# A four-layer graph network in one kernel: order of emission held on four engines, LSTM gates from Tanh alone

## The chip, the cores and the metric

The kernel runs on one core of one Trainium2 chip. The metric is the device time of one execution in microseconds; the time before is 2408.22 us, the median of three runs (2407.28 to 2410.26). Lower is better. All data are float32.

A core has a TensorE (PE in the profile; its weight loads are shown as PEld), which multiplies matrices from SBUF into PSUM; a VectorE (DVE), a ScalarE (ACT) and a GpSimd (POOL), which work element by element; and a SyncE (SP), whose queue issues most of the DMAs here. Each engine takes its instructions in the order of its own queue, and an instruction that needs another engine's result waits on a semaphore.

## The reference

The input is 128 graphs of 64 nodes with 256 features each, and one adjacency matrix. Four layers follow; each ends in `x = layernorm(x + layer(x))`.

- **Layer 0**: nodes are mixed by a normalised adjacency, then 256 to 512 features, a batch norm over all graphs and nodes, ReLU, 512 to 256, and a second batch norm. The batch norms need all data before any of it can go on.
- **Layer 1**: nodes are mixed by a scaled Laplacian, a linear map, layernorm (g1, be1), ReLU and residual; attention with four heads; layernorm (g2, be2); a feed-forward part with GELU; layernorm (g3, be3). The Laplacian is scaled by its largest eigenvalue, which the kernel finds by repeated squaring.
- **Layer 2**: two graph convolutions, and then four passes of LSTMs over windows of the 64 nodes: for p = 1, 2, 3, 4 in turn, each window of p consecutive nodes is run through an LSTM with weights of its own, and the result replaces the window's last node.
- **Layer 3**: graph attention with one head.

The LSTM step, cut to what the change touches:

```python
g = x_t @ Wih.T + h @ Whh.T + bias
i, f, gg, o = jnp.split(g, 4, axis=-1)
c = jax.nn.sigmoid(f) * c + jax.nn.sigmoid(i) * jnp.tanh(gg)
h = jax.nn.sigmoid(o) * jnp.tanh(c)
```

## The kernel before

**Tiling.** The data are 16 blocks of 512 rows (8 graphs of 64 nodes), each a tile of 128 x 1024 elements. Two layouts are in use: rows on the partitions (four pieces of 128 x 256) or features on the partitions (two pieces of 128 x 512). PSUM holds four tiles of 128 x 1024; SBUF holds the blocks and eight further tiles of that size, and tiles of blocks that are done are lent out as further ones.

**The planner.** All work is written as Python generators, one for each block or unit of work, which run while the kernel is built. Before each step a generator yields `step(engine, us, ...)` with the step's engine (T, V, S, G for TensorE, VectorE, ScalarE, GpSimd; Q for a DMA), a length in us from a table of costs written by hand, and the PSUM and SBUF tiles that it takes. `flow` (line 130) keeps a planned time for each engine. From all generators in progress it picks the step that could start first, where a step counts as ready only when its inputs have been due for a margin (line 30: 2.0 us for T, 0.5 for V and S), and among equals the one of the stream with the lowest priority number. It then lets that generator emit its instructions. The order of emission is thus the planner's order. Before the queues are filled, the framework under the kernel sorts the instructions once more, so an engine's queue need not be in the order of emission.

A step on the ScalarE whose `tbl` differs from the last one is planned 1.3 us longer, for the load of another table of functions: the three in use are named "gelu", "exp" and "sigmoid".

**Streams.** A first `flow` does layer 0 (`first_block`, `second_block`, between them the batch norms) and the eigenvalue (`eig`). A second `flow` does all the rest, with several streams side by side, each with a width (generators at a time) and a priority: `end_block` (the end of layer 0) and `block` (layer 1) in one stream of width 6; `gcn_block` (the convolutions and the LSTM for p = 1) of width 2; the LSTM units for p = 2 to 4 of width 2, except the last three, which have a stream of their own with width 1, priority 1.5 and `urgent`, which sets the margin aside; the weights' loads; and layer 3 (`last_block`) for the first 12 blocks with priority 6 and, cut into eight half blocks, for the last 4 blocks with priority 2. The last three units are the last group of graphs for p = 4, in two halves, and the group before it.

**Layernorm** comes in three forms. All begin with `stats` (line 265): for each of four pieces a `bn_stats` (L272) and a `bn_aggr` (L273), then one addition of epsilon (L274), all on the VectorE; then GpSimd raises the variance to the power -0.5.

- `ln_steps` (without weights) applies it on the VectorE (L285).
- `ln_affine_steps` (with weights; GpSimd at L294) applies it on the VectorE with two instructions for each piece, L297 and L300.
- `ln_steps_act` (GpSimd at L308) has one small VectorE instruction (L311) for minus mean times factor, and applies it on the ScalarE, one instruction for each piece (L314).

In `block` the layernorms g1 and g3 use the second form, g2 the first, and the last one the third.

**LSTM.** `lstm` (line 1025) does the first step of a window, where there is no h yet: the matmuls at L1055, the gates on the ScalarE with Sigmoid or Tanh (L1067), the product of i and g on GpSimd (L1086), tanh of the cell on the ScalarE (L1094), and the product with o on the VectorE (L1102, or straight into the block at L1357 and L1389). Later steps of whole units use a form of Strassen's scheme with seven products of half size (L1127), evictions at L1165 to L1195, gates at L1203 to L1207, a product on GpSimd (L1220) and the cell's update on the VectorE (L1228, L1231). Units of half the graphs take `plain_steps` (line 1250), with L1264 and L1266 as matmuls, L1269 as gates, L1280 on GpSimd, and L1282, L1284, L1296 on the VectorE.

**Other lines that the prediction names**: L341 the mixing of nodes, with matmuls of a quarter of the array; L353 and L359 transposes; L365 and L377 the products with weights; L749 and L772 evictions with an addition; L784 the copy of the transposed block; L808 the values; L822, L915, L916 and L933 GpSimd's additions and products with rows of weights over whole blocks; L852 a subtraction in the softmax; L898 the eviction after the attention; L928 GELU; L938 the second feed-forward product; L1325, L1345 evictions and L1353 the second ReLU in `gcn_block`; in `last_block` L1467 the copies of h, L1478 the addition of h, L1492 and L1494 copies, L1507 the product with the weights, L1519 an eviction, L1536 to L1540 the scores, L1544 the exponentials, L1555 a copy.

## Time and profile before

| what | us |
|---|---|
| median of three runs | 2408.22 |
| profiled execution | 2409.44 |
| its span, first to last instruction | 2407.7 |
| TensorE busy | 2287.2 |
| VectorE busy | 1287.7 |
| ScalarE busy | 1187.4 |
| GpSimd busy | 591.7 |

The profile comes from one execution. A row of a group reads: line, engine, operation, what it writes and reads (with the numbers of tiles left out), sizes as partitions x elements, how often; then its busy time and the mean length of one in ns; then the engine's idle time just before and what ended it. A row of waits reads: the engine and its line, what it waited for, the sum in us, how often, the longest. A row of a timeline begins with the start in us from the span's start and the length. In a table of windows each row is a stretch of time with the busy time of each engine; PEclk is the mean clock that the TensorE was granted, as a share of the full one. A TensorE that shows as busy need not be at its full rate, since the ends of its instructions are modelled.

By time, the work lies so: layer 0 up to about 270 us; the end of layer 0, layer 1, the convolutions and the first LSTM pass up to about 1290; the LSTM units for p = 2 to 4 with layer 3 of the first blocks up to about 2150; the last units and the rest of layer 3 to the end.

### The profile page before, as it was taken

To read this page: it belongs to the slowest core of one execution; us is meant where nothing else is said; L and a number is where in the kernel's file an instruction comes from. 1 tells how busy PE (TensorE), PEld (TensorE's weight loads), DVE (VectorE), ACT (ScalarE), POOL (GpSimd) and SP (SyncE) were. 2 spreads that over 40 slices of the span, in tenths; PEclk is the share of its full clock that TensorE was granted. 3 is DMA by queue.
4 is the path that set the end of the run, shared out by engine and by line. 5 is a ranking of instruction groups with operands and counts; after the bars stand their busy time and mean duration, and the time that the engine had idled before them with its cause. 6 is when DMAs were issued, how large, how long until landed. Compare 5 with 4: busy or idle time off the path is not lost.

```text
span 2407.7 us, 40603 instructions
## 1 busy us (share of the span) xinstructions
PE 2287.2 (95%) x16916; PEld 1759.9 (73%) x16916; DVE 1287.7 (53%) x2904; ACT 1187.4 (49%) x2189; POOL 591.7 (25%) x441
## 2 busy tenths in 40 slices
PE   8999788999989999999999999999999999998997
PEld 4548665666665666666667788899999888887785
DVE  4557678566483474744643433454444444455546
ACT  2257643544434544335453443444444653468766
POOL 0012134232242232331321222222221222122122
PEclk9999899999999999999999999999999999999998
DMA  6100301000000000001000000000001000001111
GB/s 162 49 1 1 111 23 49 28 10 10 1 12 17 10 10 10 1 10 36 36 19 27 18 1 1 17 2 1 1 1 36 1 10 9 19 27 66 40 36 45
DMA packets 42633, 57.91 MB, mean 24 GB/s; under 512 B 6224, under 2 KB 35536, under 8 KB 42448
## 3 DMA queue, kind: packets, MB, share of 16 engines
q1 hardware_dynamic: 41344, 54.22, 7.0%
q8 instruction: 133, 2.18, 0.4%
q10 hardware_dynamic: 1104, 1.08, 0.1%
q14 instruction: 52, 0.43, 0.1%
HBM read 38.52 MB, written 16.78 MB: 23 GB/s over the span
## 4 chain that ended last, share of the span: by engine, by line
PE 60%; DVE 16%; ACT 7%; POOL 3%; issue 2%; POOLq 0%; ACTq 0%; DVEq 0%
PE ps L1127 26%; PE ps L1055 11%; PE ps L365 7%; PE ps L377 4%; PE ps L938 4%; DVE ln_st L272 3%; ACT x L314 2%; PE ps L808 2%; POOL ln_rs L308 1%; PE ps L1507 1%; DVE x L300 1%; PE ps L341 1%; DVE ln_mv L273 1%; PE ps L353 1%; DVE ln_nm L311 1%
## 5 line engine op out<-in xcount | busy, mean ns | idle before, releaser
L1127 PE MATMUL ps<-x,x 128*128 128x256 f32 x928 | 225.0, 380 | 0.7 <-DVE t L1195 0.7
L1127 PEld LDWEIGHTS ps<-x,x 128*128 128x128 f32 x928 | 173.5, 190 | 24.9 <-issue 1.6
L314 ACT ACTIVATE x<-x,ln_nm,ln_rs 128x256 f32<-128x256 f32 x212 | 112.3, 592 | 133.3 <-DVE ln_nm L311 131.9
L1127 PE MATMUL ps<-t,x 128*128 128x256 f32 x672 | 163.7, 380 | 0.0
L1127 PEld LDWEIGHTS ps<-t,x 128*128 128x128 f32 x672 | 126.4, 190 | 17.1 <-DVE x L1195 0.8
L308 POOL TENSOR_TENSOR ln_rs<-ln_rs,neghalf 128x4 f32<-128x4 f32 (+1 forms) x72 | 71.2, 990 | 212.0 <-DVE ln_rs L274 186.4
L365 PE MATMUL ps<-t,W1T 128*128 128x512 f32 x256 | 117.8, 607 | 0.0
L1055 PE MATMUL ps<-h,wL 128*128 128x192 f32 (+2 forms) x480 | 103.9, 371 | 4.8 <-ACT h L1353 4.8
L272 DVE BATCH_NORM_STATS2 ln_st<-x 128x6 f32<-128x256 f32 x260 | 99.7, 403 | 0.4
L1055 PEld LDWEIGHTS ps<-h,wL 128*128 128x128 f32 x480 | 75.6, 192 | 29.9 <-issue 22.5
L294 POOL TENSOR_TENSOR ln_rs<-ln_rs,neghalf 128x4 f32<-128x4 f32 x32 | 36.9, 1153 | 217.1 <-DVE ln_rs L274 217.0
L1055 PE MATMUL ps<-h,x 128*128 128x256 f32 x384 | 86.7, 380 | 2.2 <-ACT t L1067 1.8
L1067 ACT ACTIVATE t<-ps,bih 128x512 f32<-128x512 f32 (+3 forms) x98 | 57.2, 634 | 55.8 <-PE ps L1055 55.1
L1203 ACT ACTIVATE x<-x,bih 128x512 f32<-128x512 f32 (+2 forms) x69 | 44.6, 648 | 80.3 <-DVE x L1193 80.0
L1186 DVE COPY x<-ps 128x256 f32<-128x256 f32 (+2 forms) x69 | 26.1, 378 | 108.4 <-PE ps L1127 107.6
L365 PEld LDWEIGHTS ps<-t,W1T 128*128 128x128 f32 x256 | 47.6, 195 | 49.6 <-issue 49.5
L365 PE MATMUL ps<-t,wA 128*128 128x512 f32 x160 | 76.8, 626 | 5.5 <-ACT t L784 5.5
L1055 PEld LDWEIGHTS ps<-h,x 128*128 128x128 f32 x384 | 72.6, 190 | 12.9 <-ACT t L1067 2.2
L1186 DVE COPY t<-ps 128x256 f32<-128x256 f32 (+2 forms) x51 | 18.8, 373 | 103.8 <-PE ps L1127 103.5
L1067 ACT ACTIVATE x<-ps,bih 128x512 f32<-128x512 f32 (+3 forms) x86 | 51.5, 650 | 40.6 <-PE ps L1055 40.4
L273 DVE BATCH_NORM_AGGREGATE ln_mv<-ln_st 128x2 f32<-128x6 f32 x448 | 71.3, 167 | 0.0
L1193 DVE TENSOR_TENSOR x<-ps,x 128x512 f32<-128x512 f32 (+2 forms) x69 | 41.4, 602 | 53.0 <-PE ps L1127 43.6
(714 smaller groups left out, 5713.2 us busy)
## 6 DMA issues: line engine op xcount, KB each, us to landing
t<-in_x_dram SPq DMA_DIRECT2D x26, 512.0 KB, 4.3
xd<-x SPq DMA_DIRECT2D x16, 512.0 KB, 2.6
x<-xd SPq DMA_DIRECT2D x8, 512.0 KB, 3.3
out_dram<-x SPq DMA_DIRECT2D x8, 512.0 KB, 2.9
h<-in_x_dram SPq DMA_DIRECT2D x5, 512.0 KB, 5.2
wL<-in_L_gnn_Wih_dram SPq DMA_DIRECT2D x2, 1024.0 KB, 5.0
x<-in_L_gnn_Whh_dram SPq DMA_DIRECT2D x2, 1024.0 KB, 5.4
x<-xd SPq DMA_DIRECT2D x5, 256.0 KB, 2.9
```

The lines of the kernel that those rows point to most:

```text
L272: V.bn_stats(st[:, t, :], y[:, t, :])
L273: V.bn_aggr(mv[:, t, :], st[:, t, :])
L308: G.tensor_tensor(rs, rs, neghalf[:, :n], ALU.pow)
L314: S.activation(y[:, t, :], y[:, t, :], AF.Identity, scale=rs[:, t : t + 1], bias=nm[:, t : t + 1])
L365: T.matmul(ps[:, c, :], w[:, k, (off + c) * P : (off + c + 1) * P], yT[:, k, :], start=(k == 0), stop=(k == nk - 1),)
L377: T.matmul(ps[:, t, :], yT[:, k, t * P : (t + 1) * P], w[:, k, :], start=(k == 0), stop=(k == nk - 1),)
L808: T.matmul(pv[r * N : (r + 1) * N, b, :, :], x1T[:, k, b * N : (b + 1) * N], Wv_par[:, k, r, :, :], start=(k == 0), stop=(k == 1),)
L938: T.matmul(tm(PS[ps])[:, t, :], fm(mem[gs[k // 2]])[:, k % 2, t * P : (t + 1) * P], W2[:, k, :], start=(k == 0), stop=(k == 3),)
L1055: T.matmul(spread(fm(PS[ps])[:, j, :n], q), WL[p][0][:, k, m], x_of(0, q)[:, k], start=(k == 0), stop=(k == 1),)
L1067: S.activation(of(sl)[:, j], fm(PS[ps])[:, j, :n], AF.Tanh if g == 2 else AF.Sigmoid, bias=bias(g, c))
L1127: T.matmul(dst, WS[p][name](k, g), y[:, k], start=first and k == 0, stop=k == 1, skip_group_check=not first)
L1186: V.tensor_copy(y[:, 1, :], v[:, 0, :])
```

## The change

1. **Order held.** `tc.manual_schedule` for TensorE, VectorE, ScalarE and GpSimd: the framework's sorting is off for these four, and each queue is in the order of emission. SP isn't among them.
2. **The planner.** The margin for T is 0.5 instead of 2.0 in the second flow. Its clocks start at the time at which the first flow ended. Many lengths are changed by some per cent. Steps have further marks: on the VectorE "m" for an instruction with two inputs from SBUF, on GpSimd "m" for one over a large tile; a VectorE step marked "m" is planned no earlier than the end of the last GpSimd step marked "m". On the TensorE a change between forms of matmul ("quarter", "columns", or neither) is planned 0.1 us longer. There is a list `DRAWS` with which margins can be multiplied by drawn numbers; it is empty, and every factor is 1.
3. **Layernorms g1 and g3** use `ln_steps_act`, followed by one multiplication and one addition over the whole block; `ln_affine_steps` is gone.
4. **LSTM.** Sigmoid of z is computed as (1 + tanh(z/2))/2, with the halves left out: the cell and h are kept at twice their value. A gate is Tanh with a scale of 0.5 or 1, halved again where the inputs are doubled; a product with a gate is (gate + 1) times the other, in one instruction; the cell's update has a factor of 0.5. All products are on the VectorE, and GpSimd keeps only differences. The bias is scaled once, in `gcn_rows`. `last_block` takes half of h.
5. **Streams.** The last three units are in the common stream of the units (width 2, priority 5), and the half blocks of the last group have priority 5.5 instead of 2.

```diff
-MARGIN = {"T": 2.0, "V": 0.5, "S": 0.5}
+MARGIN = {"T": 0.5, "V": 0.5, "S": 0.5}
+STRETCH = 50.0
+DRAWS = []
...
+    E = mybir.EngineType
+    ctx.enter_context(tc.manual_schedule(engines={E.PE, E.DVE, E.Activation, E.Pool}))
...
+                if e == "V" and tbl == "m":
+                    t, soon = max(t, locked), max(soon, locked)
...
-            if tbl is not None and tbl != table:
+            if e == "S" and tbl is not None and tbl != table:
                 us, table = us + 1.3, tbl
+            if e == "T" and tbl != shape:
+                us, shape = us + 0.1, tbl
+            if e == "G" and tbl == "m":
+                locked = when + us
...
-        yield step("V", 2.45)
+        yield step("V", 2.43)
         mv, rs = stats(y)
...
-    def ln_affine_steps(y, g, b):
-
-        yield step("V", 2.45)
-        mv, rs = stats(y)
-        yield step("G", 1.0)
-        G.tensor_tensor(rs, rs, neghalf[:, :NT], ALU.pow)
-        yield step("V", 3.4)
-        for t in range(NT):
-            V.scalar_tensor_tensor(y[:, t, :], y[:, t, :], mv[:, t, 0:1], g, ALU.subtract, ALU.mult)
-            o = b if len(b.shape) == 2 else b[:, t, :]
-            dst = y if len(b.shape) == 2 else b
-            V.scalar_tensor_tensor(dst[:, t, :], y[:, t, :], rs[:, t : t + 1], o, ALU.mult, ALU.add)
...
-        yield step("V", 0.6 * n)
+        yield step("V", 0.3 + 0.53 * n)
         mv, rs = stats(y)
...
-        yield from ln_affine_steps(y, rows[:, names.index("g1"), :], rows[:, names.index("be1"), :])
-        yield step("V", 1.25)
+        yield from ln_steps_act(y)
+        yield step("V", 3.7, tbl="m")
+        V.tensor_tensor(y, y, row["g1"], ALU.mult)
+        V.tensor_tensor(y, y, row["be1"], ALU.add)
         V.scalar_tensor_tensor(y, y, 0.0, x, ALU.max, ALU.add)
...
-        yield from ln_affine_steps(y, rows[:, names.index("g3"), :], x)
+        yield from ln_steps_act(y)
+        yield step("V", 2.45, tbl="m")
+        V.tensor_tensor(y, y, row["g3"], ALU.mult)
+        V.tensor_tensor(x, y, x, ALU.add)
...
-    V.tensor_tensor(bl, bl, bh, ALU.add)
...
+        V.tensor_tensor(bl, bl, bh, ALU.add)
+        for j in (slice(0, 4), slice(6, 8)):
+            V.tensor_scalar(bl[:, :, j], bl[:, :, j], 0.5, None, ALU.mult)
         mark("rows")
...
+        def gate(dst, z, g, c):
+            S.activation(
+                dst,
+                z,
+                AF.Tanh,
+                bias=bl[:, p - 1, 2 * g + c : 2 * g + c + 1],
+                scale=(1.0 if g == 2 else 0.5) * (1.0 if p == 1 else 0.5),
+            )
+
+        def times(dst, y, z):
+
+            V.scalar_tensor_tensor(dst, y, 1.0, z, ALU.add, ALU.mult)
...
-            t = yield step("G", g_us, at=t, waits=False)
-            G.tensor_tensor(of(s_cell)[:, c], of(sl)[:, 0], of(sl)[:, 1], ALU.mult)
+            t = yield step("V", v_us, at=t, waits=False, tbl="m")
+            times(of(s_cell)[:, c], of(sl)[:, 0], of(sl)[:, 1])
...
-            t_g = yield step("G", 2 * g_us, at=at[2], waits=False)
-            G.tensor_tensor(of(act[2]), of(act[0]), of(act[2]), ALU.mult)
+            t_g = yield step("V", 2 * v_us, at=at[2], waits=False, tbl="m")
+            times(of(act[2]), of(act[0]), of(act[2]))
...
-            V.tensor_tensor(cell, cell, of(act[2]), ALU.add)
+            V.scalar_tensor_tensor(cell, cell, 0.5, of(act[2]), ALU.mult, ALU.add)
...
-        V.tensor_tensor(x, px, x, ALU.add)
+        V.scalar_tensor_tensor(x, px, 0.5, x, ALU.mult, ALU.add)
...
-            Stream(4, 2, end),
+            Stream(4, 5.5, end),
             Stream(2, 3, gcn),
             Stream(6, 4, seq),
-            Stream(2, 5, units[:-3]),
-            Stream(1, 1.5, units[-3:], urgent=True),
+            Stream(2, 5, units),
             Stream(4, 6, last),
         ],
         MARGIN,
+        start=done["bn2",],
```

## The prediction

> **What bounds the kernel now.** I read the busy times first, then a table of windows cut where the picture changes, then what the TensorE waited for, and last the timelines around those waits. The profiled execution took 2409.4 us, 2407.7 of it span; the sum below is made against it, and it stands 1.2 us above the median of the runs, 2408.2.
>
> ```profile
> PE 2287.2 (95%) x16916; PEld 1759.9 (73%) x16916; DVE 1287.7 (53%) x2904; ACT 1187.4 (49%) x2189; POOL 591.7 (25%) x441
> ```
>
> ```profile
> core 0: us, PE busy (x) PEld busy (x) DVE busy (x) ACT busy (x) POOL busy (x), PEclk, DMA share, GB/s
> 270.00:430.00 160.00, 133.79 (x1272) 97.86 (x1273) 121.42 (x304) 83.79 (x123) 56.79 (x36) 0.90 0.17 52
> 430.00:660.00 230.00, 224.32 (x2264) 149.47 (x2263) 128.22 (x288) 109.63 (x141) 71.48 (x43) 0.99 0.04 13
> 660.00:740.00 80.00, 72.02 (x709) 46.89 (x705) 55.55 (x119) 33.94 (x44) 29.11 (x17) 0.94 0.04 14
> 960.00:1060.00 100.00, 90.64 (x987) 63.68 (x977) 74.36 (x137) 41.21 (x50) 43.23 (x24) 0.97 0.03 12
> 1290.00:1860.00 570.00, 568.71 (x3166) 515.25 (x3165) 250.37 (x449) 248.63 (x560) 127.35 (x91) 1.00 0.03 8
> 2150.00:2360.00 210.00, 195.01 (x1247) 161.77 (x1245) 111.72 (x385) 161.31 (x371) 42.01 (x51) 0.99 0.15 50
> 2360.00:2407.70 47.70, 30.17 (x208) 22.55 (x208) 28.23 (x124) 33.31 (x86) 10.14 (x16) 0.86 0.15 51
> ```
>
> The change removes no matmul, so only the 120 us in which the TensorE is idle, and the time at a lowered clock, can be won. From 270 to 1290 us (layers 1 and the start of 2) it is idle for 57.9 us, and three stretches that make a third of that time hold 43.6 of them: 26.2, 8.0 and 9.4. There the VectorE is busy for 76, 69 and 74%, against 53% in the rest, and PEclk falls to 0.90, 0.94 and 0.97. From 1290 to 2150 the TensorE is idle for under 5 us: the LSTM stage gives nothing. From 2150 on it is idle for 32.5 us, 17.5 of them in the last 47.7; the ScalarE is at 77% until then and at 70% in the last stretch.
>
> In the middle stage the TensorE's longest waits are for the VectorE and ScalarE (us, times, longest):
>
> ```profile
> PE ps L365 <- ACT t L784: 5.5, 1, 5.5
> PE ps L938 <- DVE t L898: 5.5, 1, 5.5
> PE ps L1055 <- ACT h L1353: 4.8, 2, 4.3
> ```
>
> The last of these, at 722 us, goes back to this (timelines of VectorE and GpSimd: start, length, group):
>
> ```profile
> 710.07 5.85 DVE L300 SCALAR_TENSOR_TENSOR x<-x,ln_rs,x 128x256 f32<-128x256 f32 x4 [0.51 <-POOL ln_rs L294]
> ```
>
> ```profile
> 710.01 2.34 POOL L822 TENSOR_TENSOR x<-x,rows 128x1024 f32<-128x1024 f32 x1
> 712.32 2.53 POOL L916 TENSOR_TENSOR h<-h,rows 128x1024 f32<-128x1024 f32 x1
> ```
>
> Four instructions whose usual length is 0.47 us each take 5.85 together while two GpSimd products run. Then the VectorE does another block's statistics before the eviction at L1345 on which the ReLU L1353 and the TensorE wait.
>
> **The change, part by part.**
>
> **Layernorm with weights.** Two of a block's layernorms (g1, g3) now go through the ScalarE. Removed per layernorm: eight VectorE instructions, L297 and L300. In 270 to 1290 these took 70.7 + 81.0 = 151.6 us for 32 layernorms, 4.74 each (3.8 at their medians of 0.474 and 0.48). Added: one L311 (0.43 with its stalls, 0.16 without) and two 128x1024 operations at 1.22 (L852 with two SBUF inputs: median 1.22, mean 1.36), 2.8 together; four L314 on the ScalarE at 0.592, 2.37. VectorE: 32 x 1.9 = 61 us less. ScalarE: 76 us more, hidden: it is busy for 472 of these 1020 us. A layernorm's own path is no shorter (4.74 before; 0.2 + 2.37 + 2.44 and one more hand-over after), so the gain is VectorE time only, not latency.
>
> **LSTM.** Products of gates go from GpSimd to VectorE: L1086, 1.27 us for 128x512, becomes about 0.69 (row L1102); L1220, 2.39, becomes 1.22 (row L1228); L1280, 0.73, becomes 0.42 (row L1282). In 270 to 1290 that is 32 x 0.69 = 22 us more VectorE and 41 us less GpSimd. The later ones stand under a TensorE that is 99% busy: 0; without that cover each would shorten its step by the difference, about 1 us in 24 cell updates. The doubled values cost nothing: every one of those instructions keeps its size and engine (a multiply becomes a three-operand form; 128x256 takes 0.42 either way, L1538 and L1536). The three small instructions that bring the bias to its new form (0.19 and twice about 0.16) are in a step that ends long before the first LSTM product at 453 us.
>
> **Order held.** In the profile the VectorE's order is not that of the code, where every L273 follows its own L272:
>
> ```profile
> 400.98 0.74 DVE L272 BATCH_NORM_STATS2 ln_st<-x 128x6 f32<-128x256 f32 x2
> 401.64 0.16 DVE L273 BATCH_NORM_AGGREGATE ln_mv<-ln_st 128x2 f32<-128x6 f32 x1
> 401.72 0.39 DVE L272 BATCH_NORM_STATS2 ln_st<-x 128x6 f32<-128x256 f32 x1
> 402.03 0.16 DVE L273 BATCH_NORM_AGGREGATE ln_mv<-ln_st 128x2 f32<-128x6 f32 x1
> ```
>
> One L272 always lies between, and so L273 starts 0.08 us before the instruction ahead of it ends. Where an instruction reads what the one just ahead wrote (L273 to L274, L1536 to L1538), it starts 0.035 after that end. Held order makes all 448 pairs such neighbours: 0.117 each, 0.47 per layernorm, and the evictions queued behind them (L749, L1345) come later by as much, with the TensorE waiting for those. The Trainium skill (VectorE: DVE Perf Modes, The DRAIN you can't avoid) says that the next operation waits for the pipe to empty anyway and that semaphores add nothing; by that this costs 0. The rows differ, and I take them: 320 pairs in 270 to 1290, 37 us more VectorE. Over that stage the VectorE then comes out even: -61 + 22 + 37 = -2. In the three tight stretches it does not: L297 and L300 take 76.3 us there for 14 layernorms, 39 after; 140 pairs cost 16; four LSTM products 3; in all 18 us less. What of it reaches the TensorE lies between 0 and all; I take 10, and 3 us for the clock that stays up (bounds 0 and 8).
>
> What the new order itself is worth is not in this trace. The code now keeps VectorE instructions with two SBUF inputs off GpSimd's long ones, counts the change of matmul shape, and lets a matmul group be chosen when its inputs are due 0.5 us ahead instead of 2.0. If nothing is better, 0; at best the other 48 us of idle time in this stage; at worst a loss (below). I take a third, 15, nearer to nothing, because the TensorE's waits are spread over 27 places. Layer 0 has no L272 and the same steps: 0. LSTM stage: 0, bounds -5 and +10.
>
> **Tanh alone.** Of 79 table loads 31 serve a sigmoid and 16 serve the exponentials of the last layer between them; 28 of the 29 after 2100 go.
>
> ```profile
> L1544 ACT ACT_TABLE_LOAD x14 | 18.0, 1283 | 3.2 <-DVE mx L1540 3.0
> L1269 ACT ACT_TABLE_LOAD x10 | 12.8, 1283 | 0.2
> ```
>
> ```profile
> 2158.49 1.28 ACT L1544 ACT_TABLE_LOAD   x1
> 2159.79 0.35 ACT L1544 ACTIVATE t<-t,mx 128x64 f32<-128x64 f32 x1
> ```
>
> The page ScalarE: Activation LUTs (What ACT_TABLE_LOAD costs) adds a drain of 1.38 us to each load; here the load follows an activation that ends 0.02 before and the next starts 0.02 after it, so 28 loads are 36 us, not 74. Its table of sets puts tanh beside exp, which the change needs; no run here shows it. In layer 1 it spares 16 to 32 more, off the path. At the end the ScalarE falls from 194.6 to about 161 of 257.7 us (26 of the loads lie there). The TensorE's waits for the ScalarE after 2150 sum to 12.2; half, 6. Three loads (2361.95, 2364.04, 2388.74) lie after or beside the last LSTM step: 3.8. The clock: 1. Longer statistics in two last layernorms: +0.5. Together -10; bounds -22 and +26.
>
> **The last units in the common stream.** They issue no DMA. They lose their rank over the last layer's blocks, whose loads (2.9 us) and stores go on SP, which is not held. What is queued behind them is the last four half blocks: counted as 0, priced below.
>
> Sum: -10 - 3 - 15 - 10 = -38; 2409.4 - 38 = 2371.4, which is 2370 beside the median.
>
> **Rivals.**
>
> **A much better order.** If held order with the lock counted takes most of the idle time of the middle stage, its 48 more rather than 15, and its short waits under the matmuls' tails, 30 us beside: 2370 - 33 - 30, about 2310. For it: the 5.85 and other rows like it (5.06 at 360 us) come from one kind of collision. Against: the statistics' 37 us.
>
> **Nothing.** Gains on VectorE and ScalarE stay off the path and the order is as good as before: 2408. For it: the VectorE's sum is even.
>
> **Slower: the TensorE waits at the head of its queue.** In 270 to 1290 some 330 groups of matmuls are handed over (14 for each of 16 blocks of layer 1, 16 transposes that close layer 0, 7 for each of about 13 blocks of layer 2). A group chosen with 0.5 us in hand waits when the VectorE is later than planned, and all behind it wait too. The forecast's 38 us are gone at 0.12 us per group; at 0.2 they become 66 of loss: 2370 + 66 = 2436. For it: VectorE lengths scatter (L300 from 0.46 to 2.59). Against: fewer such instructions remain.
>
> **Slower at the end.** If the two halves of the last unit finish together, eight half blocks remain instead of four; each has 6.4 us of ScalarE work (two L1467 at 0.63, four L314 at 0.59, and 2.75 in the rest), so 26 later: 2396. Alone that is not slower.
>
> **How the numbers follow.** The forecast 0.52 (its own range 2335 to 2400), the better order 0.17, nothing 0.09, slower 0.22. About 0.2%, 5 us, is what a measurement here can tell from no change. Faster 0.69, same 0.09, slower 0.22. The range 2300 to 2432 leaves about one in ten on either side.
>
> **What would show it.** L272 alternating with L273 at a 0.035 gap; no L297 or L300; in 270 to 430 TensorE idle under 20 us; one table load after 2100; ScalarE under 165 us after 2150. Wrong: new TensorE waits of 1 to 3 us in many places in the middle stage, idle time in the LSTM stage, or more than 45 us from the last LSTM matmul to the end.

## The result and the profile after

The kernel after takes 2375.57 us (median; 2374.1 to 2376.41), beside 2407.75 for the kernel before on the same chip: a ratio of 0.9864 (95% interval 0.9847 to 0.9881), 32 us less. The forecast was 2370, with 38 us less.

First the busy times of the whole profiled execution of the kernel after, then its windows, cut as those of before (window, length, busy time of each engine and its instructions, granted clock, DMA share, GB/s):

```profile
PE 2271.3 (96%) x16916; PEld 1753.3 (74%) x16916; DVE 1363.9 (58%) x2865; ACT 1161.7 (49%) x2255; POOL 432.6 (18%) x322
```

```profile
core 0: us, PE busy (x) PEld busy (x) DVE busy (x) ACT busy (x) POOL busy (x), PEclk, DMA share, GB/s
270.00:430.00 160.00, 142.96 (x1497) 105.66 (x1497) 128.42 (x298) 101.69 (x156) 55.12 (x36) 0.92 0.15 46
430.00:660.00 230.00, 227.18 (x2127) 150.08 (x2129) 152.51 (x290) 115.63 (x168) 66.34 (x38) 1.00 0.03 10
660.00:740.00 80.00, 79.90 (x718) 51.32 (x708) 46.74 (x72) 34.59 (x46) 21.26 (x13) 1.00 0.02 8
...
960.00:1060.00 100.00, 100.00 (x922) 65.42 (x922) 64.30 (x106) 46.83 (x66) 15.15 (x9) 1.00 0.09 33
...
1290.00:1860.00 570.00, 558.25 (x3045) 505.06 (x3044) 277.48 (x534) 249.39 (x578) 56.64 (x45) 1.00 0.03 8
...
2320.00:2371.20 51.20, 29.92 (x247) 21.87 (x245) 31.03 (x124) 27.44 (x86) 10.10 (x15) 0.77 0.16 54
```

The three tight stretches are nearly full: the TensorE was idle there for 26.2, 8.0 and 9.4 us, and is now for 17.0, 0.1 and 0.0. But the row 1290 to 1860, where it had been idle for 1.3 us, now has 11.8. By stage, the kernel before:

```profile
270.00:1290.00 1020.00, 962.10 (x8888) 645.68 (x8889) 609.22 (x1339) 471.85 (x623) 318.04 (x195) 0.97 0.06 22
1290.00:2150.00 860.00, 855.16 (x4787) 769.75 (x4786) 383.50 (x758) 400.42 (x906) 195.46 (x143) 1.00 0.03 8
2150.00:2407.66 257.65, 225.18 (x1455) 184.32 (x1453) 139.94 (x509) 194.62 (x456) 52.15 (x67) 0.97 0.15 50
```

And the kernel after:

```profile
270.00:1290.00 1020.00, 996.15 (x9232) 680.93 (x9232) 645.65 (x1243) 513.69 (x754) 282.63 (x165) 0.99 0.06 20
1290.00:2150.00 860.00, 834.93 (x4703) 749.84 (x4702) 431.83 (x894) 395.49 (x950) 92.62 (x78) 1.00 0.03 11
2150.00:2371.21 221.21, 194.73 (x1180) 160.38 (x1178) 131.25 (x426) 130.25 (x342) 32.38 (x43) 0.94 0.14 46
```

Length less PE busy is the idle time. The middle stage goes from 57.9 to 23.9 us; the LSTM stage, which was full, goes from 4.8 to 25.1; the end goes from 32.5 to 26.5. With layer 0 the idle time falls from 120.5 to 99.9. The other 15.9 of the 36.5 us between the two spans is matmul time: as many matmuls take 2271.3 instead of 2287.2. The granted clock accounts for it. In these two traces it is at every moment 1 or 0.5, and 68.0 us of the matmul time before, but only 36.3 after, lie in stretches at 0.5 (windows cut where the clock changes). Half the clock is about half the rate: in the kernel before, the transposes L353 and L359 start 0.109 us apart at the one and 0.214 at the other. So 34.0 and 18.1 us are lost, a difference of 15.9. The mean over the whole span, 0.982 and 0.986, shows less of it, because the last stretch at 0.5 in the kernel after, 14.8 us long, has the TensorE busy for 3.1 us only. (The matmul time at full clock that is left is 2253 us in both and between 2245 and 2263 in the runs below, so the account is good to some us, not to a tenth.)

So the total is close to the forecast, but the LSTM stage, for which it had nothing, lost 20 us. These are the TensorE's largest waits between 1290 and 2150 in the kernel after (sum in us, times, longest; L1153 is a matmul of the LSTM's seven-product steps, L1049 a gate, L1221 a sum ahead of a gate, L1199 one of the differences; L1532 and L1578 are matmuls of the last layer):

```profile
PE ps L1153 <- DVE x L1221: 3.4, 6, 1.8
PE ps L1153 <- ACT x L1049: 2.7, 5, 0.7
PE ps L1532 <- ACT t L1049: 2.0, 2, 1.0
PE ps L1578 <- DVE t L1199: 1.6, 1, 1.6
PE ps L1153 <- ACT t L1049: 1.3, 3, 0.5
```

No wait is long. There are 39 pauses above 0.1 us in that stage, 24.6 us together, where the kernel before has 11 with 4.7.

### The profile page after: what moved, and what is told of

Read it like the earlier page. It is cut to its first block, busy times and chain, and to the rows that moved or that the text cites. A ratio compares the mean times of both kernels' runs of the same rounds, so it can differ in the third digit from the quotient of the medians.

```text
span 2371.2 us, 40454 instructions
## 1 busy us (share of the span) xinstructions
PE 2271.3 (96%) x16916; PEld 1753.3 (74%) x16916; DVE 1363.9 (58%) x2865; ACT 1161.7 (49%) x2255; POOL 432.6 (18%) x322
## 4 chain that ended last, share of the span: by engine, by line
PE 79%; issue 8%; DVE 7%; ACT 4%; POOL 0%; DMA 0%; ACTq 0%; POOLq 0%; DVEq 0%
PE ps L1153 26%; PE ps L1081 14%; PE ps L370 11%; PE ps L382 6%; PE ps L945 4%; PE ps L645 3%; PE ps L1532 2%; PE ps L815 2%; PE ps L346 2%; PE ps L1291 2%; PE ps L1289 2%; DVE ln_st L290 1%; PE ps L358 1%; DVE ln_mv L291 1%; PE ps L1588 1%
## 5 line engine op out<-in xcount | busy, mean ns | idle before, releaser
L313 POOL TENSOR_TENSOR ln_rs<-ln_rs,neghalf 128x4 f32<-128x4 f32 (+1 forms) x104 | 106.6, 1025 | 661.5 <-DVE ln_rs L292 546.5
L1153 PE MATMUL ps<-t,x 128*128 128x256 f32 x832 | 203.5, 380 | 1.7 <-DVE x L1221 1.1
L1153 PEld LDWEIGHTS ps<-t,x 128*128 128x128 f32 x832 | 155.9, 190 | 25.9 <-issue 2.7
L1049 ACT ACTIVATE t<-ps,bih 128x512 f32<-128x512 f32 (+5 forms) x191 | 102.8, 578 | 140.7 <-PE ps L1081 111.2
L1153 PE MATMUL ps<-x,x 128*128 128x256 f32 x672 | 166.4, 380 | 0.7 <-DVE x L1221 0.4
L1153 PEld LDWEIGHTS ps<-x,x 128*128 128x128 f32 x672 | 124.4, 190 | 16.2 <-DVE x L1221 1.2
L1049 ACT ACTIVATE x<-ps,bih 128x512 f32<-128x512 f32 (+5 forms) x153 | 77.8, 539 | 110.3 <-PE ps L1081 77.6
L290 DVE BATCH_NORM_STATS2 ln_st<-x 128x6 f32<-128x256 f32 x240 | 96.1, 401 | 0.6
L1081 PEld LDWEIGHTS ps<-h,wL 128*128 128x128 f32 x480 | 74.2, 190 | 22.6 <-issue 21.3
L291 DVE BATCH_NORM_AGGREGATE ln_mv<-ln_st 128x2 f32<-128x6 f32 x448 | 81.5, 182 | 15.3
L1049 ACT ACTIVATE x<-x,bih 128x512 f32<-128x512 f32 (+5 forms) x134 | 68.5, 559 | 40.2 <-DVE x L1219 37.7
L370 PEld LDWEIGHTS ps<-t,W1T 128*128 128x128 f32 x256 | 46.7, 190 | 48.8 <-issue 48.5
L316 DVE SCALAR_TENSOR_TENSOR ln_nm<-ln_mv,ln_rs 128x4 f32<-128x4 f32 (+1 forms) x104 | 63.0, 609 | 33.2 <-POOL ln_rs L313 33.0
L1212 DVE COPY x<-ps 128x256 f32<-128x256 f32 (+2 forms) x67 | 25.2, 375 | 92.7 <-PE ps L1153 92.4
L1049 ACT ACTIVATE t<-t,bih 128x512 f32<-128x512 f32 (+2 forms) x98 | 50.5, 563 | 55.7 <-DVE t L1219 53.6
```

The source lines that it names most:

```text
L290: V.bn_stats(st[:, t, :], y[:, t, :])
L291: V.bn_aggr(mv[:, t, :], st[:, t, :])
L313: G.tensor_tensor(rs, rs, neghalf[:, :n], ALU.pow)
L316: V.scalar_tensor_tensor(nm, mv[:, :, 0], -1.0, rs, ALU.mult, ALU.mult)
L370: T.matmul(ps[:, c, :], w[:, k, (off + c) * P : (off + c + 1) * P], yT[:, k, :], start=(k == 0), stop=(k == nk - 1),)
L1049: S.activation(dst, z, AF.Tanh, bias=bl[:, p - 1, 2 * g + c : 2 * g + c + 1], scale=(1.0 if g == 2 else 0.5) * (1.0 if p == 1 else 0.5),)
```

## The experiments

The table has the TensorE's idle time by stage in the profiled execution of each run, its busy time for the same 16916 matmuls and the mean granted clock. Ratios are to the kernel before on the chip of that run; an interval reaches 0.0009 to 0.0018 to either side. The stages are stretches of time, not of work: a slower run is less far on when a stretch ends.

| kernel | median us | ratio | 0-270 | 270-1290 | 1290-2150 | 2150-end | PE busy | clock |
|---|---|---|---|---|---|---|---|---|
| before | 2407.75 | 1 | 25.3 | 57.9 | 4.8 | 32.5 | 2287.2 | 0.982 |
| after | 2375.57 | 0.9864 | 24.5 | 23.9 | 25.1 | 26.5 | 2271.3 | 0.986 |
| 1 before, order held | 2427.57 | 1.0081 | 24.7 | 44.9 | 29.8 | 34.7 | 2291.4 | 0.977 |
| 2 after, not held | 2443.48 | 1.0139 | 26.3 | 82.4 | 9.9 | 25.0 | 2289.2 | 0.976 |
| 3 after, margin 2.0 | 2378.46 | 0.9876 | 26.5 | 27.6 | 28.4 | 26.9 | 2267.7 | 0.986 |
| 4 after, sigmoid | 2389.72 | 0.9924 | 25.5 | 23.9 | 31.5 | 27.2 | 2278.4 | 0.985 |
| 5 after, held to 1300 | 2350.49 | 0.9760 | 26.7 | 24.0 | 7.8 | 27.5 | 2263.4 | 0.988 |
| 6 after, statistics apart | 2361.03 | 0.9803 | 25.0 | 18.9 | 23.8 | 23.7 | 2264.9 | 0.989 |
| 7 after, layernorm as before | 2393.12 | 0.9939 | 25.5 | 38.2 | 23.8 | 26.5 | 2278.7 | 0.981 |
| 8 after, last units urgent | 2406.69 | 0.9993 | 25.2 | 24.0 | 41.8 | 28.0 | 2285.4 | 0.984 |
| 9 as 5, TensorE held on | 2371.70 | 0.9848 | 25.2 | 23.9 | 21.5 | 30.0 | 2267.9 | 0.988 |
| 10 as 5, last units urgent | 2358.09 | 0.9788 | 27.1 | 24.0 | 8.4 | 27.4 | 2268.8 | 0.988 |
| 11 after, two rules out | 2372.12 | 0.9851 | 25.0 | 27.1 | 22.7 | 26.5 | 2270.6 | 0.984 |
| 12 edits of 5 and 6 | 2340.21 | 0.9719 | 25.3 | 18.4 | 8.1 | 25.2 | 2261.0 | 0.988 |

The theory that I began with: holding the order fills the middle stage, and the TensorE's smaller margin costs the LSTM stage. Rivals: the planner's new rules fill the middle stage, and the gate products on the VectorE cost the LSTM stage; or the holding itself costs it.

### 1. The kernel before with its order held

```diff
+    E = mybir.EngineType
+    ctx.enter_context(tc.manual_schedule(engines={E.PE, E.DVE, E.Activation, E.Pool}))
```

> The kernel before with its order of emission held on the four engines, and nothing else of the change. Theory H (the holding itself brings the gain of the middle stage): TensorE idle from 270 to 1290 us falls from 58 to 30 or less, time about 2385. Rival R (the new rules of the planner bring it: the lock, the shape of matmuls, 0.5 us of margin; holding alone only adds the statistics' 0.117 us gaps, 37 us of VectorE there): idle stays at 50 to 65, time 2400 to 2425. Idle of the LSTM stage (1290 to 2150): by H and R under 8, as before, if the 0.5 margin or the products on VectorE are what costs the 20 us there; about 25 if the holding costs them.

It is 19.5 us slower than before. The windows of this run:

```profile
270.00:1290.00 1020.00, 975.14 (x9021) 662.14 (x9022) 653.47 (x1344) 477.00 (x629) 319.31 (x197) 0.97 0.06 22
1290.00:2150.00 860.00, 830.21 (x4538) 743.29 (x4537) 378.68 (x743) 380.57 (x876) 188.27 (x138) 1.00 0.02 8
```

The middle stage wins 13 us of idle time although its VectorE is busy 44 us longer. That lies between the two theories. The LSTM stage loses 25 us, with the margin still at 2.0 and the products still on GpSimd (188 us busy, 195 before): holding alone does it. Most of that lies late in the stage:

```profile
1860.00:2000.00 140.00, 127.42 (x733) 111.03 (x731) 62.82 (x150) 69.76 (x163) 33.56 (x26) 1.00 0.01 5
2000.00:2150.00 150.00, 142.05 (x748) 126.88 (x749) 73.24 (x147) 70.53 (x157) 29.36 (x23) 0.99 0.03 11
```

From 1860 to 2150 the TensorE is idle here for 20.5 us, in the kernel before for 3.6. This run still has the last three units in their urgent stream, which runs 8 and 10 look at.

### 2. The kernel after with nothing held

```diff
-    ctx.enter_context(tc.manual_schedule(engines={E.PE, E.DVE, E.Activation, E.Pool}))
```

> The kernel after with nothing held: the same stream of instructions as emitted, put in order as before's was. Theory H: most of the middle stage's gain goes, idle of 270 to 1290 from 24 to 45 or more, time 2390 to 2405. Rival R (order as emitted is what counts, held or not): within 5 us of 2376. In both the pairs L290 to L291 lose their gap where another instruction is put between. If the holding costs the LSTM stage its 20 us, idle there falls from 25 to under 8.

It is 66 us slower than after by the ratios (the profiled execution was 9 us faster than the other three), far beyond both theories. The two stages go opposite ways:

```profile
270.00:1290.00 1020.00, 937.56 (x8805) 634.06 (x8806) 567.71 (x1182) 482.67 (x696) 270.89 (x162) 0.96 0.06 20
1290.00:2150.00 860.00, 850.07 (x4786) 756.23 (x4785) 433.51 (x881) 407.64 (x936) 93.03 (x78) 1.00 0.04 12
```

In the middle stage 82.4 us are idle, 58.5 more than in the kernel after; in the LSTM stage 9.9, 15 fewer. Runs 1 and 2 together: held order saves 13 us of idle time in the middle stage with the old stream of work and 58 with the new one, and it costs 25 and 15 in the LSTM stage. What makes the new stream so dependent on being held was not taken apart further.

### 3. The margin back at 2.0

```diff
-MARGIN = {"T": 0.5, "V": 0.5, "S": 0.5}
+MARGIN = {"T": 2.0, "V": 0.5, "S": 0.5}
```

> The kernel after with the TensorE's margin at 2.0 us as before. Theory M (a matmul group chosen with 0.5 us in hand waits at the head of its queue, and that is the idle time of the LSTM stage): idle from 1290 to 2150 falls from 25 to under 10; in the middle stage idle changes by less than 10; time 2360 to 2372. Rival V (VectorE's products of gates are what TensorE waits for, whatever the margin): LSTM idle stays at 20 to 30, time 2370 to 2390. Rival G (the small margin is the gain of the middle stage): idle of 270 to 1290 rises from 24 to 40 or more, time above 2390.

Theory M falls: the LSTM stage is idle for 28.4 us, not under 10. So does G: the middle stage has 27.6. The time, 0.9876 beside 0.9864, can't be told from that of the kernel after. By its numbers this is rival V's row, but run 1 had already shown that V's cause, the products on the VectorE, isn't needed for the loss.

### 4. Sigmoid back

```diff
-                AF.Tanh,
+                AF.Tanh if g == 2 else AF.Sigmoid,
```

> The kernel after, in the same order of emission, with Sigmoid in place of Tanh for gates i, f and o: as many instructions of the same size, other values (so the output is not the reference's), and the table loads come back. Forecast's step: about 28 loads after 2100, 36 us of ScalarE there, of which 9 to 11 us reach the end: about 2386. Rival (loads are hidden): 2374 to 2379. Rival (in a held order a load stands ahead of whatever is queued on ScalarE, and nothing can go around it): 20 us or more, 2396 and above, part of it before 2100, where 16 to 32 loads would come back too.

It costs 14 us (0.9924 beside 0.9864), a little over the forecast's step, but not where the forecast had it: the idle time after 2150 grows by less than 1 us. There are 59 table loads instead of 17: 18 more before 1290, which leave the idle time there at 23.9; 9 between 1850 and 2100; 15 after 2100, where the forecast had 28. Of the 15.3 us between the two spans 6.4 are idle time of the LSTM stage and 7.1 matmul time. This is how one of its waits comes about (timeline of the TensorE in this run: start, length, what, and the idle time before it):

```profile
2044.33 0.66 PE L1153 MATMUL ps<-x,wA 128*128 128x144 f32 x4
2048.57 0.76 PE L1153 MATMUL ps<-h,wL 128*128 128x144 f32 x4 [3.58 <-ACT x L1049]
```

The ScalarE's timeline up to it:

```profile
2043.37 1.28 ACT L1569 ACT_TABLE_LOAD   x1
...
2045.91 0.19 ACT L1569 ACTIVATION_READ_ACCUMULATOR t<-t,mx 128x1 f32 x1
2046.11 1.28 ACT L1049 ACT_TABLE_LOAD   x1
2047.41 0.84 ACT L1049 ACTIVATE x<-x,bih 128x288 f32<-128x288 f32 x2
2048.16 0.36 ACT L1049 ACTIVATE x<-ps,bih 128x144 f32<-128x144 f32 x1
```

The exponentials of a last-layer block stand ahead of the gates; the load on either side of them, 2.56 us together, is, as an estimate, most of what holds the gates back in a wait of 3.58: from the first load to the gates the timeline shows no pause of the ScalarE. Before the exponentials the load starts 0.02 us after the activation before it ends, as in the kernel before; no further drain shows.

### 5. Held up to the LSTM stage only

```diff
-    ctx.enter_context(tc.manual_schedule(engines={E.PE, E.DVE, E.Activation, E.Pool}))
+    held = tc.manual_schedule(engines={E.PE, E.DVE, E.Activation, E.Pool})
+    held.__enter__()
+    holds = [held]
...
             end, now = when + us, when
+            if holds and now > 1300.0:
+                holds.pop().__exit__(None, None, None)
```

> The kernel after, in the same order of emission, held only for what is emitted before the plan's time of 1300 us (about where the LSTM stage begins); what comes later is put in order as in the kernel before. Theory L (holding gains in the middle stage and costs in the LSTM stage): TensorE idle of 270 to 1290 stays at 20 to 28, idle of 1290 to 2150 falls from 25 to 10 or less, time 2352 to 2364, faster than both. Rival B (the emitted order of the end was planned to be held, and freed it puts the last layer's work late): idle of the LSTM stage falls, but what follows it grows by as much, time 2372 to 2395.

Here 1300 is the planner's own time; what is emitted later is sorted by the framework as in the kernel before. The run takes 2350.49 us, 25 less than after (0.9760 beside 0.9864), from the same order of emission:

```profile
270.00:1290.00 1020.00, 996.00 (x9228) 680.32 (x9227) 646.99 (x1244) 513.54 (x753) 282.74 (x165) 0.99 0.06 21
1290.00:2150.00 860.00, 852.24 (x4824) 770.26 (x4823) 439.54 (x915) 411.36 (x970) 94.38 (x81) 1.00 0.04 12
2150.00:2349.41 199.41, 171.93 (x1073) 141.32 (x1071) 112.68 (x406) 123.05 (x323) 29.61 (x40) 0.95 0.14 46
```

The middle stage is that of the kernel after. The LSTM stage's idle time falls to 7.8 us, with the VectorE as busy there as in the kernel after (440 beside 432 us), so theory L holds and V is out. The end doesn't grow: idle 27.5 beside 26.5, and the time that the freed order wins in the LSTM stage is kept.

### 9. From 1300 on, the TensorE alone held

```diff
                 holds.pop().__exit__(None, None, None)
+                ctx.enter_context(tc.manual_schedule(engines={E.PE}))
```

> As the kernel held up to the plan's 1300 us (2350.5 us, TensorE idle 7.8 us from 1290 to 2150), but from there on the TensorE alone is held, the three others are put in order as before. Theory T (what costs is the TensorE's held order: a group of matmuls stands at the head before its inputs are there, and nothing goes around it): idle of the LSTM stage 18 us or more, time 2362 to 2378. Rival E (what costs is the held order of the evictions and cell updates on ScalarE and VectorE, whose lateness the TensorE only shows): idle under 12, time 2346 to 2357.

21 us of the 25 come back as loss (0.9848 beside 0.9760), and 21.5 us of idle time are in the LSTM stage:

```profile
1290.00:2150.00 860.00, 838.46 (x4727) 756.39 (x4726) 432.75 (x895) 406.86 (x956) 91.66 (x79) 1.00 0.04 11
```

Theory T holds: the held order of the TensorE's own queue alone is enough for most of the cost. The other way round, the three others held and the TensorE free, was not tried. With ScalarE and VectorE free the pauses are as many and as short as in the kernel after: 34 above 0.1 us, the longest 2.0, beside 39, longest 1.8. With the TensorE free too there are 14.

### 8 and 10. The last three units back in a stream of their own

```diff
-            Stream(4, 5.5, end),
+            Stream(4, 2, end),
...
-            Stream(2, 5, units),
+            Stream(2, 5, units[:-3]),
+            Stream(1, 1.5, units[-3:], urgent=True),
```

> The kernel after with the last three LSTM units in their own urgent stream and the last half blocks at rank 2, as before the change. Forecast's step (the move is worth 0): 2371 to 2381. Rival (the common stream lets both halves of the last unit end together, so the old form ends sooner): the end from the last LSTM matmul shrinks by 10 or more, 2350 to 2366. Rival (the move is what shortened the end): TensorE idle after 2150 rises from 26 to 35 or more, 2385 and above.

> As the kernel held up to the plan's 1300 us, with the last three LSTM units in their own urgent stream and the last half blocks at rank 2, as before the change. In the order held to the end that cost 31 us, 17 of them as TensorE idle from 1860 to 2150. Theory C (the urgent stream is only bad where the order is held; where it is not, as in the kernel before, other work goes around its waits, so that the forecast's 0 was right for the order it was made for): 2345 to 2360. Rival (the order of the work itself is worse, held or not): 2370 to 2385, idle of 1860 to 2150 at 15 or more.

In the kernel after, this takes back nearly the whole gain: 0.9993 beside 0.9864, 31 us. Until 1860 the two are alike. The two windows that follow, in the kernel after:

```profile
1860.00:2000.00 140.00, 134.22 (x790) 118.39 (x789) 72.56 (x155) 63.04 (x166) 18.12 (x15) 1.00 0.05 18
2000.00:2150.00 150.00, 142.46 (x873) 126.38 (x871) 81.79 (x208) 83.06 (x206) 17.85 (x18) 1.00 0.05 17
```

In run 8:

```profile
1860.00:2000.00 140.00, 127.24 (x661) 108.17 (x661) 61.83 (x113) 56.33 (x136) 15.47 (x12) 1.00 0.01 4
2000.00:2150.00 150.00, 132.76 (x742) 114.56 (x740) 71.75 (x157) 66.00 (x165) 15.95 (x16) 0.97 0.06 18
```

The TensorE is idle here for 30.0 us instead of 13.3, and 260 of its matmuls are left for later. Of the 30.0, waits for the LSTM's gates (L1049) make 18.1; in the kernel after they make 6.6 of the 13.3. Of the 33.1 us between the two spans 19.0 are idle time and 14.1 matmul time, of which half clock, reckoned as above, explains some 4; the rest is open. Where the LSTM stage is not held, the same edit costs 7 us (run 10 beside run 5, 0.9788 and 0.9760), and 5.0 us are idle in that stretch. So theory C holds for most of it: the old streams are bad where the order is held, and where it isn't, the sorting finds other work for the TensorE. That it is the urgent stream's matmuls, ahead of their gates, is what the waits suggest; which of the two edits, the stream or the rank of the half blocks, does more was not tried apart. The late part of run 1's loss lies in the same place.

### 6. The statistics put apart

```diff
         for t in range(n):
             V.bn_stats(st[:, t, :], y[:, t, :])
+        for t in range(n):
             V.bn_aggr(mv[:, t, :], st[:, t, :])
```

> The kernel after with the four L290 of a layernorm ahead of its four L291; steps and their prices as before, so the plan is the same. Forecast's step (an instruction that reads what the one just ahead wrote starts 0.117 us later): the 448 gaps of +0.034 us become about -0.083, 52 us less of VectorE's time, 37 of them from 270 to 1290. What that is worth on TensorE: a third of the 24 us idle there or less, time 2366 to 2376. Rival (by the price of a pipe that empties after every instruction): gaps and time unchanged, 2374 to 2378.

It is 15 us faster than after (0.9803 beside 0.9864), more than the step expected. Part of one layernorm's statistics in the VectorE's timeline of the kernel after:

```profile
410.98 0.39 DVE L290 BATCH_NORM_STATS2 ln_st<-x 128x6 f32<-128x256 f32 x1
411.41 0.18 DVE L291 BATCH_NORM_AGGREGATE ln_mv<-ln_st 128x2 f32<-128x6 f32 x1
411.51 0.40 DVE L290 BATCH_NORM_STATS2 ln_st<-x 128x6 f32<-128x256 f32 x1
```

All of it in this run, where like neighbours are shown as one row (x4):

```profile
405.45 1.40 DVE L290 BATCH_NORM_STATS2 ln_st<-x 128x6 f32<-128x256 f32 x4
406.77 0.36 DVE L292 BATCH_NORM_AGGREGATE ln_mv<-ln_st 128x2 f32<-128x6 f32 x4
407.17 0.17 DVE L293 TENSOR_SCALAR ln_rs<-ln_mv 128x4 f32<-128x4 f32 x1
```

In the kernel after each L291 starts 0.034 us after the end of the L290 that it reads (411.37 to 411.41); here the first starts 0.08 before the last L290 ends (406.77, 406.85), and the four of them (L292 in this run) take 0.36 together instead of 0.18 each. The whole VectorE is busy for 1314.5 us instead of 1363.9, 49 less, of which 46.7 are in the three lines of the statistics, against 52 forecast; the rival, by which such gaps cost nothing, is out. Of the 15 us, 5.0 are idle time of the middle stage, 2.8 of the end, 6.4 matmul time (the mean clock goes from 0.986 to 0.989).

### 7. The layernorms g1 and g3 as before

```diff
-        yield from ln_steps_act(y)
-        yield step("V", 3.7, tbl="m")
-        V.tensor_tensor(y, y, row["g1"], ALU.mult)
-        V.tensor_tensor(y, y, row["be1"], ALU.add)
+        yield from ln_affine_steps(y, rows[:, names.index("g1"), :], rows[:, names.index("be1"), :])
+        yield step("V", 1.25, tbl="m")
...
-        yield from ln_steps_act(y)
-        yield step("V", 2.45, tbl="m")
-        V.tensor_tensor(y, y, row["g3"], ALU.mult)
-        V.tensor_tensor(x, y, x, ALU.add)
+        yield from ln_affine_steps(y, rows[:, names.index("g3"), :], x)
```

> The kernel after with the layernorms g1 and g3 back on VectorE alone (eight operations of three operands each, in place of four on ScalarE and the products and sums of 128x1024); all else of the change stays, the planner's prices as before the change. Forecast's step (18 us of VectorE in the tight stretches, 10 of them on TensorE, 3 for the clock): 2385 to 2393. Rival (VectorE's length is off the path, latency counts and is no shorter): 2370 to 2380. Rival (in a held order VectorE's length counts in full): 61 us more in the middle stage, 2400 and above, TensorE idle there 45 or more.

The definition of `ln_affine_steps` is put back too. It costs 18 us (0.9939 beside 0.9864): in the profiled executions, which are 21 apart, 14.3 of idle time in the middle stage and 7.4 of matmul time at a clock of 0.981. The forecast's two terms, 10 and 3, were the right ones and somewhat small. The planner makes another order with these steps, so that a part of the 18 may be order is not excluded. The window of the middle stage:

```profile
270.00:1290.00 1020.00, 981.85 (x9142) 669.12 (x9141) 670.23 (x1388) 450.80 (x617) 282.39 (x163) 0.98 0.06 21
```

The VectorE is busy for 670 us, 25 more than in the kernel after, not 61, since this stage is less far on when the window ends (90 matmuls fewer) and since in the kernel after another instruction takes time back: `ln_nm`, 128x4 (72 of them and 23.8 us in this run). Its group in the kernel after (count, busy time, mean ns of one, and idle time before it):

```profile
L316 DVE SCALAR_TENSOR_TENSOR ln_nm<-ln_mv,ln_rs 128x4 f32<-128x4 f32 (+1 forms) x104 | 63.0, 609 | 33.2 <-POOL ln_rs L313 33.0
```

GpSimd's timeline where one of them is long:

```profile
424.71 2.37 POOL L829 TENSOR_TENSOR h<-h,rows 128x1024 f32<-128x1024 f32 x1
```

The VectorE's at the same place:

```profile
424.77 2.33 DVE L316 SCALAR_TENSOR_TENSOR ln_nm<-ln_mv,ln_rs 128x4 f32<-128x4 f32 x1 [1.18 <-POOL ln_rs L313]
```

An instruction whose median is 0.157 us lasts as long as the GpSimd product that started just ahead of it. 104 of them take 63.0 us; at the median it would be 16.3. In 26 of them the end comes about 0.02 us after the end of a GpSimd product that had started first, and these 26 take 50.2 of the 63.0. The planner's new rule doesn't see these: their step carries no mark.

### 11. Without two of the planner's rules

```diff
-                if e == "V" and tbl == "m":
-                    t, soon = max(t, locked), max(soon, locked)
...
-            if e == "T" and tbl != shape:
-                us, shape = us + 0.1, tbl
```

> The kernel after without two rules of its planner: the one that keeps VectorE instructions marked m off GpSimd's marked ones, and the 0.1 us for a change of matmul shape; all else as after, order held to the end. Theory P (they make the order good, which holding alone did not: with holding alone 45 us of TensorE idle stayed from 270 to 1290): idle there rises from 24 to 35 or more, VectorE busy rises by 10 or more with instructions of 1 us and longer where the median is under 0.5, time 2388 to 2400. Rival (the rules move little): idle 20 to 30, time 2370 to 2384.

0.9851 beside 0.9864: no difference that can be told. The rival holds. The VectorE is busy for 1351.6 us, 12 less, so theory P is wrong in its sign too: with the rule out, fewer of the small instructions fall under GpSimd's long ones (the 104 `ln_nm` take 45.6 us, 17.4 less).

### 12. The two edits that gained, together

> The two edits that made the kernel after faster, together: order held only up to the plan's 1300 us (2350.5 alone, 25.1 us less than after) and the four L290 of a layernorm ahead of its four L291 (2361.0 alone, 14.5 less). If they are independent, the sum: 2375.6 - 25.1 - 14.5 = 2336. The first acts from 1290 on and the second mainly before, where 11 of its matmul time was won; but behind 1290 the freed order already had another L290 between some of the pairs, so that part of the second is lost: 2336 to 2344. Rival (with the VectorE shorter, the freed part is put in another order and the end grows): 2345 to 2356.

The edits are those of runs 5 and 6. 2340.21 us, ratio 0.9719 (0.9706 to 0.9732): 67.6 us less than the kernel before and 35 less than the kernel after, 5 short of the sum of the two, within the first theory's range.

```profile
270.00:1290.00 1020.00, 1001.58 (x9249) 683.88 (x9250) 609.17 (x1246) 517.55 (x760) 282.08 (x165) 0.99 0.06 20
1290.00:2150.00 860.00, 851.91 (x4842) 773.41 (x4841) 441.30 (x925) 411.45 (x978) 95.31 (x81) 1.00 0.04 13
```

Each stage keeps its own gain: 18.4 us idle in the middle stage as in run 6, 8.1 in the LSTM stage as in run 5.

## Why the prediction came out right, and which of its steps didn't

The time is 5.6 us from the forecast and well inside the likeliest case's own range, but the sum came out partly by luck. The forecast's 38 us were 25 of idle time in the middle stage, 0 in the LSTM stage, 9 at the end and 4 for the clock. Measured are 34.0 in the middle stage, a loss of 20.2 in the LSTM stage, 6.0 at the end and 15.9 for the clock (and 0.8 in layer 0). The middle stage and the clock gave 21 us more than forecast, and the LSTM stage took as much away.

The two steps that were counted as nothing do not cancel either. Run 10 has neither of them, the order held past 1300 and the last units moved, and has all the rest: it is 51 us faster than before. With both the kernel after is 18 us slower than that. What each is worth depends on the other: holding past 1300 costs 49 us with the old streams (runs 10 and 8) and 25 with the new (runs 5 and after); moving the units gains 31 where the order is held and 7 where it isn't.

Each effect below is what the kernel after loses when that part is taken out; the planner makes a new order for some of these runs, and parts that help one another count twice, so they needn't add up to the 32.

- **Layernorm with weights** (forecast 10 + 3): 18. Right in place, some 5 us too small, and the mechanism fits. The sum by which the VectorE came out even over the middle stage (-2) was wrong: it is busy there for 36 us more than before, with 4% more matmuls in that stretch. One reason is `ln_nm` (L311 before), priced at 0.43 us at most, which takes 0.61 on the mean and 36 us more than before in all.
- **The gap behind an instruction that is read next** (0.117 us, 448 pairs): shown. All 448 pairs stand at +0.033 to +0.035 us in the trace of after; in that of before the 281 L273 right behind an L272 of another piece start 0.083 ahead of its end; the busy time in run 6 fell by 49 where 52 were worked out. The rule of the Trainium skill (VectorE: DVE Perf Modes, The DRAIN you can't avoid) that the next operation waits until the pipe is empty, which the prediction set aside for the rows, would by itself have made run 6 no faster. The same section adds that a next operation that is not held starts earlier, which the prediction left out and which the starts 0.083 us ahead agree with. The prediction took this cost off the layernorm's gain as VectorE time; taken out, it was worth 15 us on its own.
- **Order held** (forecast -15, "LSTM stage: 0, bounds -5 and +10"): this is the step that failed. Holding has two effects of opposite sign in two stages. In the middle stage it saved 13 us of idle time with the old stream of work and 58 with the new; in the LSTM stage it cost 25 and 15 to 17, beyond the bound of 10. The prediction gives no reason for its 0 there but that the stage was 99% busy, as if that were a property of the work. It was owed to the framework's order, which the change put out of use: run 1 changes nothing else. Why the new stream depends on being held so much more in the middle stage stays open.
- **The rival of a TensorE that waits at the head of its queue** had the mechanism right (run 9) and the place and cause wrong: not in the middle stage and not through the 0.5 us of margin, which makes no difference (run 3), but in the LSTM stage, where the waits are for gates and sums.
- **What the new order is worth** ("a third" of 48 us, 15): the middle stage has 34 us less idle time in all, the layernorms' part included. Two of the planner's rules and the margin, taken out, make no difference that can be told from zero (runs 11 and 3); holding does (run 2).
- **Tanh alone** (forecast 10): 14, right in size and not in place: the forecast had nearly all of it at the end, and run 4 has 6.4 us as idle time of the LSTM stage and less than 1 after 2150. No load follows 2100 in the kernel after, where one was expected: its only load after layer 1 is at 1893 us. In 270 to 1290 the loads fall from 47 to 15, and run 4 shows that the 18 that return there cost no idle time. That the gates' Tanh never causes a load, neither after GELU nor after an exponential, is seen in the 17 loads of the kernel after, none of which is at a gate (L1049): 418 gates follow a load for GELU as the last one, 248 one for an exponential.
- **The last units** ("They issue no DMA ... counted as 0", priced at 26 as a loss): a gain of 31 in held order. The prediction looked at what stands behind the last units, the last layer's blocks; the loss is in the TensorE's own queue from 1860 to 2150, in waits for gates. Where nothing is held behind 1300, 0 was not far off: run 10 gives 7.
- **Clock** (forecast 3 + 1): 15.9 of the 36.5 us between the spans, four times the forecast. The direction was right and the size was not: between 310 and 1290 the kernel before has eight stretches at 0.5, the kernel after one.

Of the signs named beforehand, all on the right side came but the one load after 2100, which stayed away too: the alternation at 0.035 us, no L297 or L300, 17.0 us idle from 270 to 430, ScalarE at 130 us after 2150. Of those on the wrong side two came as well, idle time in the LSTM stage and more than 45 us from the last LSTM matmul to the end: 67.2 (2304.0 to 2371.2), where the kernel before has 38.4. The second does not show as harm, since the last layer's blocks fill most of it (26.5 us idle after 2150, 32.5 before): from 2320 on the TensorE is idle for 21.3 us, before in its last 47.7 for 17.5.

## What to carry to other kernels

An engine that shows no idle time may owe that to the order that something else made; when a change takes that order away, bound its loss by how the work is chained, not by how busy the stage was. Try where to hold an order and where to let go: here the same stream of work was 25 us faster with its second half released, and a run with the TensorE alone held showed that its queue is enough for most of the loss. Two parts of a change that both touch the order should be tried together and apart, as the last units and the holding were. Where one instruction reads what its neighbour has just written, put another between: one added line was worth 15 us on an engine that was busy for 58% of the time.

## What the runs showed of the hardware that was not expected

A VectorE instruction of 128x4 elements, 0.157 us at its median, takes up to 2.33 us when a GpSimd product of 128x1024 starts just ahead of it; in the kernel after some 46 us of VectorE time go to this (the 26 that end with such a product take 50.2, at the median 4.1). The granted clock went with the idle time: 0.977 and 0.976 in the two runs with most of it (134 and 144 us), 0.986 to 0.989 in the five with least (77 to 100 us), and the same 16916 matmuls took 2291 and 2289 us in the first two, 2261 to 2271 in those five. No run here sets the clock apart from the idle time, so which waits bring it down is not shown.
